# Conditional residual layer norm, 128 batches: the 1/standard-deviation chain in three VectorE steps instead of four, means made in pairs, the b2 row of ten more batches added by VectorE, and another order in the last five batches

## The chip, the core and the metric

The kernel runs on one core of a Trainium2 chip. The metric is the device time of one execution in microseconds (us). All work is in fp32, apart from three bf16 matmuls that only copy rows.

Engines: TensorE (PE in the profile, with PEld for its weight loads), VectorE (DVE), ScalarE (ACT), GpSimd (POOL). SP is the engine whose queue issues nearly all transfers.

## The reference

`x` has 128 batches of 128 rows by 512 columns. Each batch has an integer `language_id`, which picks one of ten sets of weights.

```python
w1 = W1[language_ids];  w2 = W2[language_ids]
h = relu(einsum('bsh,bha->bsa', x, w1) + b1[language_ids][:, None, :])      # 512 -> 128
adapted = einsum('bsa,bah->bsh', h, w2) + b2[language_ids][:, None, :]      # 128 -> 512
y = x + adapted
mean = jnp.mean(y, axis=-1, keepdims=True)
var = jnp.mean(jnp.square(y - mean), axis=-1, keepdims=True)
normed = (y - mean) * jax.lax.rsqrt(var + 1e-5)
out = x + normed * gamma[language_ids][:, None, :] + beta[language_ids][:, None, :]
```

## The kernel before

One batch is one tile of 128 partitions (its rows) by 512 columns. The weights of all ten languages stay on the chip. At the start one-row matmuls spread every row of `gamma`, `beta` and `b2` over the 128 partitions (`spread`), into `gamma_b`, `beta_b` and `b2_b`. The matrix `pick` selects the row, and its columns for `gamma` carry the factor 2.

One loop over `i` does all the work. Every engine gets its instructions in program order, because `keep` ties each to the one before it on its engine. In iteration `i`, with `b = i - 3`:

- PE transposes `x` of batch `i` (L231), multiplies batch `i-1` down to 128 columns (`down`, L254) and batch `i-2` up to 512 columns (`up`, L271, into the PSUM tile `py`). For some batches `up` is led by one bf16 matmul that writes the row of `b2` (L270).
- ACT copies the transposed tile to SBUF (`copy_xT`, L235), applies relu (L262), squares the residual tile of batch `b` with the sum of squares as by-product (`square`, L301), and copies the weights of a later batch into place (`stage_w1`, L222). After every odd batch it takes the square root for the pair (`deviation`, L312).
- POOL adds `b2` to `x` for most batches two ahead (`add_b2`, L241) and `beta` to `x` for every batch (`add_beta`, L248).
- DVE adds the residual, with the row sum as by-product (`residual`, L286), makes the negative mean (`negative_mean`, L292), and multiplies by gamma (`scale`, L335) and by 1/deviation while adding `x + beta` (`finish`, L344).

Where `b2` is added depends on the batch. `b2_by_matmul` names the batches where PE does it: 0 to 3, and those with `b % 4 == 1` that `b2_by_vector` does not take. `b2_by_vector` names those where DVE does it with one more instruction in front of the residual (L284): 13, 21, ..., 109. For all others POOL does it. That makes 22 batches for PE, 13 for DVE and 93 for POOL.

The reciprocal deviation of a pair takes ScalarE's root and one Heron step on DVE, in four instructions on tiles of two columns: `rstd_1` (L318, a reciprocal), `rstd_2` (L322), `rstd_3` (L326) and `rstd_4` (L330, a reciprocal). In an even step DVE runs `residual`, `rstd_1`, `scale` of the pair before, `negative_mean`, `rstd_2`, `finish` of an older batch, `rstd_3`. In an odd step it runs `b2` if it is its turn, then `residual`, `rstd_4`, `scale`, `negative_mean`, `finish`.

The tile pools set how far the engines can drift apart: `py` has five buffers, the transposed tile `pxT` one, the down product `ph` one.

The last five batches (from `E = 123`) are written out by hand in `tail`. There single batches replace pairs (`rstd_of`, `deviation_of`), two batches are finished by ACT and POOL (`by_pool`: ACT scales, POOL multiplies by gamma and adds; `shift` makes the bias that ACT needs), a third by ACT and POOL's last addition alone, and each store covers one batch (`store_last`).

Of the kernel before, what the change touches and what calls it, by code (L numbers as in the profile page):

```python
# [16 lines left out]
P = 128  # L17
# [8 lines left out]
def cond_resid_kernel(ctx: ExitStack, tc: tile.TileContext, x, itok, W1, b1, W2, b2, gamma, beta, out):  # L26
# [18 lines left out]
    def keep(ins):  # L45

        engine = ins.ins.engine
        if engine in last:
            tc.add_manual_dep(ins.ins, last[engine], behind, reason="kept order")
        last[engine] = ins.ins.name  # L50
        return ins
# [11 lines left out]
    p_y = ctx.enter_context(tc.tile_pool(name="p_y", bufs=5, space=PSUM))  # L63

    xs = {}

    def load_x(g):
        t = xp.tile([P, G, H], FP, tag="x", name=f"x_{g}")
# [26 lines left out]

    warm = const.tile([P, 1], FP, name="warm")
    keep(nc.vector.memset(warm, 1.0))
    keep(nc.scalar.activation(warm, warm, AF.Sqrt))
    def load_w1(k):
        keep(  # L100
            nc.sync.dma_start(out=w1[:, :, k, :], in_=W1[:, k * P : (k + 1) * P, :].rearrange("l p a -> p l a"))
# [15 lines left out]
    both = st.tile([P, R], FP, tag="both", name="both", bufs=1)[:96, :]  # L117
    keep(nc.vector.tensor_tensor(both, ident[:96, 0:R], ident[:96, 32 : 32 + R], ALU.add))
    keep(nc.vector.tensor_tensor(pick, both, ident[:96, 64 : 64 + R], ALU.add))
    keep(nc.vector.tensor_scalar(pick[:, L : 2 * L], pick[:, L : 2 * L], 2.0, None, ALU.mult))  # L120

    lids, w1s = {}, {}

# [7 lines left out]
    def lid(b, engine):  # L131
        g = b // G
        if (g, engine) not in lids:
            loads, vals = nc.values_load_multi_w_load_instructions(
                lang[0:1, g * G : (g + 1) * G],
                engines=[engine],
                min_val=0,
                max_val=L - 1,
                skip_runtime_bounds_check_because="clamped on the chip to 0..L-1 above",
            )  # L140
            for ins in loads:
                keep(ins)
            lids[g, engine] = vals
        return lids[g, engine][b % G]
# [66 lines left out]
    phs, pxs, sums = {}, {}, {}  # L211

    def b2_by_matmul(b):
        return b < 4 or (b % 4 == 1 and not b2_by_vector(b))

    def b2_by_vector(b):
        return b % 8 == 5 and 8 <= b < B - 16

    def stage_w1(b):
        w1s[b] = wp.tile([P, KC, A], FP, tag="w1s", name=f"w1s_{b}")  # L220
# [53 lines left out]
    def col(tiles, b):  # L274

        return tiles[b // 2][:, b % 2 : b % 2 + 1]

    def residual(b):
        r = rs.pop(b) if b in rs else xb(b)
        if b % 2 == 0:  # L280
            sums[b // 2] = st.tile([P, 2], FP, tag="sum", name=f"sum_{b // 2}")
        if b2_by_vector(b):
            v = lid(b, ET.DVE)
            keep(nc.vector.tensor_tensor(ys[b], ys[b], b2_b[:, bass.ds(v * H, H)], ALU.add))  # L284
        keep(
            nc.vector.scalar_tensor_tensor(ys[b], ys[b], 1.0, r, ALU.mult, ALU.add, accum_out=col(sums, b))  # L286
        )

    def negative_mean(b):
        if b % 2 == 0:  # L290
            nmeans[b // 2] = st.tile([P, 2], FP, tag="nmean", name=f"nmean_{b // 2}")
        keep(nc.vector.tensor_scalar(col(nmeans, b), col(sums, b), -1.0 / H, None, ALU.mult))  # L292

    def square(b):

# [7 lines left out]
            )  # L303
        )

    sds, y0s, stats = {}, {}, {}

    H3 = float(H) ** 3

    def deviation(g):  # L310
        sds[g] = st.tile([P, 2], FP, tag="sd", name=f"sd_{g}")
        keep(nc.scalar.activation(sds[g], ssqs[g], AF.Sqrt, bias=eps, scale=1.0 / H3))  # L312

    def rstd_1(g):
        y0s[g] = p_s.tile([P, 6], FP, tag="s", name=f"stat_{g}")
        keep(nc.vector.reciprocal(y0s[g][:, 0:2], sds[g]))  # L318

    def rstd_2(g):  # L320
        t = y0s[g]
        keep(nc.vector.scalar_tensor_tensor(t[:, 2:4], ssqs.pop(g), EPS * H3, t[:, 0:2], ALU.add, ALU.mult))  # L322

    def rstd_3(g):
        t = y0s[g]
        keep(nc.vector.scalar_tensor_tensor(t[:, 4:6], t[:, 2:4], 1.0 / H3, sds.pop(g), ALU.mult, ALU.add))  # L326

    def rstd_4(g):
        rstds[g] = st.tile([P, 2], FP, tag="rstd", name=f"rstd_{g}")
        keep(nc.vector.reciprocal(rstds[g], y0s.pop(g)[:, 4:6]))  # L330

    def scale(b):
        v = lid(b, ET.DVE)
# [17 lines left out]
    def on(b):  # L351
        return 0 <= b < B

    E = B - 5
    ends = {}

    def rstd_of(b, n):

        if not ends:
            ends["t"] = p_s.tile([P, 32], FP, tag="s", name="stat_ends")
        t = ends["t"][:, 8 * (b % 4) : 8 * (b % 4) + 3]
        if n == 1:
            keep(nc.vector.reciprocal(t[:, 0:1], sds[b]))
        elif n == 2:
            keep(
                nc.vector.scalar_tensor_tensor(t[:, 1:2], ssqs.pop(b), EPS * H3, t[:, 0:1], ALU.add, ALU.mult)
            )
        elif n == 3:  # L370
            keep(nc.vector.scalar_tensor_tensor(t[:, 2:3], t[:, 1:2], 1.0 / H3, sds.pop(b), ALU.mult, ALU.add))
        else:
            rstds[b] = st.tile([P, 1], FP, tag="rstd", name=f"rstd_{b}")
            keep(nc.vector.reciprocal(rstds[b], t[:, 2:3]))

    def deviation_of(b):
        ssq = st.tile([P, 1], FP, tag="ssq", name=f"ssq_{b}")
        sq = tp.tile([P, H], FP, tag="sq", name=f"sq_{b}")
        keep(nc.scalar.activation(sq, ys[b], AF.Square, bias=col(sums, b), scale=-float(H), accum_out=ssq))  # L379
        sds[b] = st.tile([P, 1], FP, tag="sd", name=f"sd_{b}")  # L380
        keep(nc.scalar.activation(sds[b], ssq, AF.Sqrt, bias=eps, scale=1.0 / H3))
        ssqs[b] = ssq

    def rstd_col(b):
        return rstds[b] if b > E else rstds[b // 2][:, b % 2 : b % 2 + 1]

    def shift(b):
        ends[b] = st.tile([P, 1], FP, tag="shift", name=f"shift_{b}")
        keep(nc.vector.tensor_scalar(ends[b], col(nmeans, b), rstd_col(b), None, ALU.mult))

    def by_pool(b, scaled):

        n = rp.tile([P, H], FP, tag="r", name=f"n_{b}")
        bias = 0.0 if scaled else ends.pop(b)
        keep(nc.scalar.activation(n, ys.pop(b), AF.Identity, bias=bias, scale=rstd_col(b)))  # L395
        if not scaled:
            keep(nc.gpsimd.tensor_tensor(n, n, gamma_b[:, bass.ds(lid(b, ET.Pool) * H, H)], ALU.mult))
        o = os[b // 2][:, b % 2, :]
        keep(nc.gpsimd.tensor_tensor(o, n, o, ALU.add))

    def store_last(b):
        nc.sync.dma_start(out=out[b], in_=os[b // 2][:, b % 2, :])

    def finish_last(b):
        o = os[b // 2][:, b % 2, :]
        keep(nc.vector.scalar_tensor_tensor(o, ys.pop(b), rstd_col(b), o, ALU.mult, ALU.add))  # L406
        store_last(b)

    def tail(b):
        p = E // 2  # L410
        if b == E + 3:
            rstd_of(b - 2, 3)
        residual(b)
        if b == E + 1:
            rstd_1(p)
            scale(E - 1)
            rstd_2(p)
            negative_mean(b)
            finish(E - 2)
            store(p - 1)  # L420
            rstd_3(p)
            deviation_of(b)
            rstd_4(p)
            shift(E)
            by_pool(E, False)
        elif b == E + 2:
            rstd_of(b - 1, 1)
            negative_mean(b)
            rstd_of(b - 1, 2)
            finish_last(E - 1)  # L430
            store_last(E)
            deviation_of(b)
        elif b == E + 3:
            rstd_of(b - 2, 4)
            shift(b - 2)
            residual(b + 1)
            by_pool(b - 2, False)
            store_last(b - 2)
            rstd_of(b - 1, 1)
            negative_mean(b)  # L440
            rstd_of(b - 1, 2)
            negative_mean(b + 1)
            scale(b - 1)
            deviation_of(b)
            rstd_of(b - 1, 3)
            rstd_of(b - 1, 4)
            scale(b)
            deviation_of(b + 1)
            by_pool(b - 1, True)
            store_last(b - 1)  # L450
            rstd_of(b, 1)
            rstd_of(b, 2)
            rstd_of(b + 1, 1)
            rstd_of(b, 3)
            rstd_of(b + 1, 2)
            scale(b + 1)
            rstd_of(b, 4)
            rstd_of(b + 1, 3)
            rstd_of(b + 1, 4)
            finish_last(b)  # L460
            finish_last(b + 1)


    def spin(n, width):
# [43 lines left out]
    for i in range(3, B + U):  # L508
# [35 lines left out]
        if b > E:  # L544
            tail(b)
        elif half == 0:
            if on(b):
                residual(b)
            if mine:
                rstd_1(p)  # L550
                scale(2 * p)
            if on(b):
                negative_mean(b)
            if mine:
                rstd_2(p)
            if old:
                finish(2 * p - 1)
                store(p - 1)
            if mine:
                rstd_3(p)  # L560
        else:
            if on(b):
                residual(b)
            if mine:
                rstd_4(p)
                scale(2 * p + 1)
            if on(b):
                negative_mean(b)
            if mine:
                finish(2 * p)  # L570
        if 0 <= b <= E:
# [46 lines left out]
```

## Time and profile before

| what | value |
|---|---|
| median of 3 runs | 312.11 us (312.1 to 312.15) |
| the profiled execution's own time | 311.92 us |
| its span, first to last instruction | 310.1 us |
| granted TensorE clock, mean | 0.988 |
| PE busy | 298.7 us, 96% of the span |
| DVE busy | 297.3 us, 96% |
| ACT busy | 280.3 us, 90% |
| POOL busy | 280.4 us, 90% |
| chain that ended last, by engine | PE 83%, DMA 8%, DVE 4% |

How to read it: a share of busy time counts time in which at least one instruction of the engine is open. An instruction's mean duration runs from its start to the end of its writes. On DVE and ACT the next instruction starts before that, so the distance between two starts in the timeline, not the duration, is what an instruction costs an engine that is full. The span plus about 1.8 us makes the time of the profiled execution.

### The profile page before, as it was taken

Reading aid. Unit: us, or ns where it says so; the run is one execution under the profiler, and the core shown is the slowest. Engines: PE = TensorE matmul, PEld = TensorE weight load, DVE = VectorE, ACT = ScalarE, POOL = GpSimd, SP = SyncE. Lnnn points to the kernel's source line nnn. Section 1 sums busy time; section 2 is a strip of 40 time slices with the busy share of each in tenths; the row PEclk is TensorE's granted clock in tenths of the full one; section 3 lists DMA queues with packets and bytes.
Section 4 is the critical chain, followed back from the end, with each engine's and each line's share of the span. In section 5 each row is a group of like instructions: output and inputs, shape, how many; then the busy total and the mean of one; then the engine's idle time right before and its main releaser. Section 6 shows DMA issues by size and latency. Waiting matters only on the chain.

```text
span 310.1 us, 7084 instructions
## 1 busy us (share of the span) xinstructions
PE 298.7 (96%) x1856; PEld 223.5 (72%) x1856; DVE 297.3 (96%) x945; ACT 280.3 (90%) x716; POOL 280.4 (90%) x234
## 2 busy tenths in 40 slices
PE   8999999999999999999999999999999999999970
PEld 3758778787777777777777777777777777777740
DVE  6778999999999999999999999999999999999995
ACT  3857999999999999999999999999999999999982
POOL 1349999999999999999999999999999999999963
PEclk9999999999999999999999999999999999999995
DMA  7999989975688667566876657577766766773234
GB/s 239 379 389 387 373 227 368 373 280 226 233 272 268 235 200 251 207 248 225 271 268 222 219 191 265 217 251 274 256 230 205 230 235 246 233 271 135 98 143 169
DMA packets 43481, 77.59 MB, mean 250 GB/s; under 512 B 1929, under 2 KB 7060, under 8 KB 43442
## 3 DMA queue, kind: packets, MB, share of 16 engines
q1 hardware_dynamic: 43382, 77.10, 71.7%
q8 instruction: 15, 0.25, 0.3%
q14 instruction: 24, 0.20, 0.2%
q10 hardware_dynamic: 60, 0.05, 0.1%
HBM read 43.58 MB, written 33.55 MB: 249 GB/s over the span
## 4 chain that ended last, share of the span: by engine, by line
PE 83%; DMA 8%; DVE 4%; ACT 1%; issue 1%; SPq 1%; DVEq 1%; ACTq 0%
PE ph L254 33%; PE py L271 32%; PE pxT L231 17%; DMA w1e<-in_L_cond_W_dram 4%; DMA x<-in_x_dram 3%; PE py L270 1%; DVE py L286 1%; DVE py L335 1%; DVE o L344 1%; SPq L152 1%; DMA ids<-in_itok_B_dram 0%; ACT sq L379 0%; DVEq L613 0%; ACT n L395 0%; DVE o L406 0%
## 5 line engine op out<-in xcount | busy, mean ns | idle before, releaser
L248 POOL TENSOR_TENSOR o<-x,beta_b 128x512 f32<-128x512 f32 x128 | 162.4, 1282 | 9.5 <-DVE beta_b L208 9.4
L254 PE MATMUL ph<-xT,w1s 128*128 128x128 f32 x1024 | 135.4, 275 | 0.0
L271 PE MATMUL py<-w,hT 128*128 x256 | 131.1, 594 | 0.0
L241 POOL TENSOR_TENSOR r<-x,b_b 128x512 f32<-128x512 f32 x93 | 119.1, 1281 | 12.5 <-DVE b_b L208 6.2
L254 PEld LDWEIGHTS ph<-xT,w1s 128*128 128x128 f32 x1024 | 125.0, 192 | 1.0 <-ACT hT L262 0.3
L231 PEld LDWEIGHTS pxT<-ident,x 128*128 128x128 f32 x512 | 66.7, 152 | 65.0 <-issue 46.4
L335 DVE SCALAR_TENSOR_TENSOR py<-py,nmean,gamma_b 128x512 f32<-128x512 f32 x126 | 93.7, 744 | 0.1
L344 DVE SCALAR_TENSOR_TENSOR o<-py,rstd,o 128x512 f32<-128x512 f32 x122 | 91.1, 747 | 0.0
L301 ACT ACTIVATE sq<-py,sum 128x512 f32<-128x512 f32 x124 | 84.8, 684 | 2.3 <-DVE py L286 2.1
L231 PE MATMUL pxT<-ident,x 128*128 128x128 f32 x512 | 77.9, 275 | 0.1
L235 ACT COPY xT<-pxT 128x512 f32<-128x512 f32 x128 | 74.9, 585 | 1.2 <-PE pxT L231 1.2
L286 DVE SCALAR_TENSOR_TENSOR py<-py,r 128x512 f32<-128x512 f32 x93 | 64.7, 695 | 1.1 <-POOL o L248 0.4
L222 ACT COPY w1s<-w 128x512 f32 x104 | 63.6, 612 | 0.0
L262 ACT ACTIVATE hT<-ph,b1T 128x128 f32<-128x128 f32 x128 | 47.1, 368 | 11.2 <-PE ph L254 7.8
L271 PEld LDWEIGHTS py<-w,hT 128*128 128x128 f32 x256 | 40.5, 192 | 2.4 <-issue 0.9
L286 DVE SCALAR_TENSOR_TENSOR py<-py,x 128x512 f32<-128x512 f32 x35 | 24.4, 697 | 2.0 <-issue 0.8
L301 ACT ACTIVATION_READ_ACCUMULATOR sq<-py,sum 128x1 f32 x124 | 25.2, 203 | 0.0
L312 ACT ACTIVATE sd<-ssq,eps 128x2 f32<-128x2 f32 x62 | 18.3, 296 | 2.1
L292 DVE TENSOR_SCALAR nmean<-sum 128x1 f32<-128x1 f32 x128 | 19.6, 153 | 0.1
L318 DVE RECIPROCAL stat<-sd 128x2 f32<-128x2 f32 x62 | 13.0, 210 | 1.5 <-ACT sd L312 1.5
L286 DVE DVE_READ_ACCUMULATOR py<-py,r 128x1 f32 x93 | 13.5, 145 | 0.0
L222 ACT COPY w1s<-w1e 128x512 f32 x16 | 9.8, 611 | 1.1 <-DMA w1e<-in_L_cond_W_dram 1.1
(56 smaller groups left out, 115.9 us busy)
## 6 DMA issues: line engine op xcount, KB each, us to landing
out_dram<-o SPq DMA_DIRECT2D x61, 512.0 KB, 3.3
x<-in_x_dram SPq DMA_DIRECT2D x29, 1024.0 KB, 6.2
x<-in_x_dram SPq DMA_DIRECT2D x6, 512.0 KB, 8.8
w1e<-in_L_cond_W_dram SPq DMA_DIRECT2D x2, 1280.0 KB, 11.5
w<-in_L_cond_W_dram SPq DMA_DIRECT2D x4, 640.0 KB, 7.9
w1s<-in_L_cond_W_dram SPq DMA_DIRECT2D x8, 256.0 KB, 8.4
w<-in_L_cond_W_dram SPq DMA_DIRECT2D x1, 1792.0 KB, 9.9
out_dram<-o SPq DMA_DIRECT2D x6, 256.0 KB, 2.0
```

The source lines that it names most:

```text
L222: keep(nc.scalar.copy(w1s[b].rearrange("p k a -> p (k a)"), src))
L231: keep(nc.tensor.transpose(pxs[b][:, k, :], cols, ident))
L235: keep(nc.scalar.copy(xT[b], pxs.pop(b)))
L241: keep(nc.gpsimd.tensor_tensor(rs[b], xb(b), b2_b[:, bass.ds(v * H, H)], ALU.add))
L248: keep(nc.gpsimd.tensor_tensor(os[g][:, j, :], xb(b), beta_b[:, bass.ds(v * H, H)], ALU.add))
L254: nc.tensor.matmul(phs[b], lhsT=w1s[b][:, k, :], rhs=xT[b][:, k, :], start=(k == 0), stop=(k == KC - 1))
L262: keep(nc.scalar.activation(hT[b], phs.pop(b), AF.Relu, bias=b1T[:, bass.ds(lid(b, ET.Activation), 1)]))
L271: keep(nc.tensor.matmul(ys[b], lhsT=hT[b], rhs=w2[:, bass.ds(v * H, H)], start=not m, stop=True))
L286: nc.vector.scalar_tensor_tensor(ys[b], ys[b], 1.0, r, ALU.mult, ALU.add, accum_out=col(sums, b))
L301: nc.scalar.activation(sq, ys[b], AF.Square, bias=col(sums, b), scale=-float(H), accum_out=col(ssqs, b))
L335: nc.vector.scalar_tensor_tensor(ys[b], ys[b], col(nmeans, b), gamma_b[:, bass.ds(v * H, H)], ALU.add, ALU.mult)
L344: nc.vector.scalar_tensor_tensor(o, ys.pop(b), rstds[g][:, j : j + 1], o, ALU.mult, ALU.add)
```

## The change

It has four parts.

1. ScalarE's function is `Abs_reciprocal_sqrt` instead of `Sqrt`, and writes into PSUM. The four DVE instructions of a pair become three (`rstd(g, 1..3)`, in `newton` and `newton_3`): with `t` the table's value and `v` the variance, `u = (ssq + eps)·t`, `u = u·t` with its scaling, `rstd = (u - 3)·t`. That is minus two times the Newton value, so `gamma` carries -0.5 instead of 2. The third instruction moves from the even step into the odd step, between DVE's `b2` addition and the residual.
2. `negative_means(g)` makes both negative means of a pair in one instruction in the odd step, in place of one `negative_mean` in each step. A column pair of zeros in PSUM is its second operand.
3. `b2` goes from PE to DVE for ten batches: 25, 41, 49, 57, 73, 81, 89, 105, 113 and 117. Batch 125 goes from PE to POOL. PE keeps 0 to 3, 5, 9, 17, 33, 65, 97 and 121 (11 batches); DVE has 23; POOL has 94.
4. In the last five batches the small operations come in another order, batch 125 is finished half by ACT and POOL (columns 0 to 255) and half by DVE (256 to 511), and each store is issued where its batch ends.

```diff
-    keep(nc.vector.tensor_scalar(pick[:, L : 2 * L], pick[:, L : 2 * L], 2.0, None, ALU.mult))
+    keep(nc.vector.tensor_scalar(pick[:, L : 2 * L], pick[:, L : 2 * L], -0.5, None, ALU.mult))
...
-        return b < 4 or (b % 4 == 1 and not b2_by_vector(b))
+        return b < 4 or (b % 4 == 1 and not b2_by_vector(b) and b < E)
...
-        return b % 8 == 5 and 8 <= b < B - 16
+        return b % 4 == 1 and (b % 8 == 5 if b < 24 else b % 32 != 1) and 8 <= b < B - 8
...
+    def smalls(lo, n):
+        if not small:
+            small["t"] = p_s.tile([P, 64], FP, tag="s", name="small")
+            keep(nc.vector.memset(small["t"][:, 0:2], 0.0))
+        return small["t"][:, lo : lo + n]
+
+    def negative_means(g):
+        nmeans[g] = st.tile([P, 2], FP, tag="nmean", name=f"nmean_{g}")
+        keep(nc.vector.scalar_tensor_tensor(nmeans[g], sums[g], -1.0 / H, smalls(0, 2), ALU.mult, ALU.add))
...
+    def root(ssq, t):
+        keep(nc.scalar.activation(t, ssq, AF.Abs_reciprocal_sqrt, bias=eps, scale=1.0 / H3))
+
+    def newton(n, ssq, t, u):
+        if n == 1:
+            keep(nc.vector.scalar_tensor_tensor(u, ssq, EPS * H3, t, ALU.add, ALU.mult))
+        else:
+            keep(nc.vector.scalar_tensor_tensor(u, u, 1.0 / H3, t, ALU.mult, ALU.mult))
+
+    def newton_3(rstd, t, u):
+        keep(nc.vector.scalar_tensor_tensor(rstd, u, -3.0, t, ALU.add, ALU.mult))
...
             if on(b):
                 residual(b)
             if mine:
-                rstd_1(p)
+                rstd(p, 1)
                 scale(2 * p)
-            if on(b):
-                negative_mean(b)
-            if mine:
-                rstd_2(p)
+                rstd(p, 2)
             if old:
                 finish(2 * p - 1)
                 store(p - 1)
+        else:
+            if on(b):
+                vector_b2(b)
             if mine:
-                rstd_3(p)
-        else:
+                rstd(p, 3)
             if on(b):
                 residual(b)
             if mine:
-                rstd_4(p)
                 scale(2 * p + 1)
             if on(b):
-                negative_mean(b)
+                negative_means(g)
             if mine:
                 finish(2 * p)
```

The end of the new `tail`, for batch 126 (`b`), with 125 as `b - 1` and 127 as `b + 1`:

```python
shift(b - 2); by_pool(b - 2, False); residual(b + 1); store_last(b - 2)
rstd_of(b - 1, 1); scale(b - 1); rstd_of(b - 1, 2); negative_means(b // 2)
deviation_of(b); scale(b); rstd_of(b - 1, 3); deviation_of(b + 1)
by_pool(b - 1, True, left)
rstd_of(b, 1); scale(b + 1); rstd_of(b, 2)
finish_cols(b - 1, right); store_last(b - 1)
rstd_of(b, 3); rstd_of(b + 1, 1); finish_cols(b); store_last(b)
rstd_of(b + 1, 2); rstd_of(b + 1, 3); finish_cols(b + 1); store_last(b + 1)
```

In `before` the same stretch was: `rstd_of(b - 2, 4)`, `shift(b - 2)`, `residual(b + 1)`, then after `scale(b)` of batches 125 and 126 one after the other all four small steps of 126 and 127 interleaved with `scale(b + 1)`, and the two `finish_last` at the end.

## Prediction

> **What bounds the kernel now.** I read the page's busy row first, then the groups by line, then the chain of waits, and last the timeline of each engine over one stretch of 5 us.
>
> ```profile
> PE 298.7 (96%) x1856; PEld 223.5 (72%) x1856; DVE 297.3 (96%) x945; ACT 280.3 (90%) x716; POOL 280.4 (90%) x234
> ...
> L270 PE MATMUL py<-parts,pick 96*128 96x512 bf16 x22 | 8.4, 381 | 0.5 <-DVE b_b L208 0.5
> ```
>
> Two engines are full, so a gain on either is capped by the other. The chain says which one leads, and what one `b2` matmul costs there:
>
> ```profile
> 144.49 0.89 PE ph L254 x8
> 145.38 0.22 PE py L270
> 145.60 0.86 PE py L271 x2
> 146.46 0.44 PE pxT L231 x4
> 146.90 0.89 PE ph L254 x8
> 147.79 0.86 PE py L271 x2
> 148.65 0.44 PE pxT L231 x4
> 149.09 0.89 PE ph L254 x8
> ```
>
> PE runs without a gap: a batch takes 2.19 (149.09 - 146.90), and 2.41 with L270. So L270 costs 0.22, not its mean duration of 0.381. DVE's timeline over the odd step of a batch whose `b2` it adds:
>
> ```profile
> 155.27 0.16 DVE L326 SCALAR_TENSOR_TENSOR stat<-stat,sd 128x2 f32<-128x2 f32 x1
> 155.34 0.69 DVE L284 TENSOR_TENSOR py<-py,b_b 128x512 f32<-128x512 f32 x1
> 156.06 0.70 DVE L286 SCALAR_TENSOR_TENSOR py<-py,x 128x512 f32<-128x512 f32 x1
> 156.68 0.14 DVE L286 DVE_READ_ACCUMULATOR py<-py,x 128x1 f32 x1
> 156.68 0.17 DVE L330 RECIPROCAL rstd<-stat 128x2 f32<-128x2 f32 x1
> 156.76 0.74 DVE L335 SCALAR_TENSOR_TENSOR py<-py,nmean,gamma_b 128x512 f32<-128x512 f32 x1
> 157.41 0.15 DVE L292 TENSOR_SCALAR nmean<-sum 128x1 f32<-128x1 f32 x1
> 157.47 0.74 DVE L344 SCALAR_TENSOR_TENSOR o<-py,rstd,o 128x512 f32<-128x512 f32 x1
> 158.13 0.69 DVE L286 SCALAR_TENSOR_TENSOR py<-py,r 128x512 f32<-128x512 f32 x1
> ```
>
> The distance between starts is the price. A small operation costs 0.06 to 0.08 (157.41 to 157.47; 156.68 to 156.76), whatever its duration of 0.15 to 0.21. Over the stretch from 60 to 280 us the odd step without L284 takes 2.05 and the even step 2.18, so a pair takes 4.235; L284 adds 0.727. A group of four batches with one L284 takes 9.20 on DVE and 8.76 on PE, and before the change such a group alternates with one that has L270 (8.47 on DVE, 8.98 on PE). Over eight batches that is 17.67 against 17.74: PE leads by a hair, and DVE waits for it at the residual. The third view is how lateness of DVE reaches PE:
>
> ```profile
> 156.86 0.69 ACT L301 ACTIVATE sq<-py,sum 128x512 f32<-128x512 f32 x1
> ...
> 158.38 0.58 ACT L235 COPY xT<-pxT 128x512 f32<-128x512 f32 x1
> ...
> 159.01 0.14 PEld L231 LDWEIGHTS pxT<-ident,x 128*128 128x128 f32 x1 [0.24 <-ACT xT L235]
> ```
>
> In that step the square waits for the residual (156.06 plus 0.61 plus the accumulator's 0.14) with only 0.04 to spare. Behind it in ACT's queue stands the copy of the transposed tile, and PE's next transposes wait for its one buffer: they start at 159.44, and their weight load of 0.14 was free at 159.01. So DVE may be late by about 0.3 (0.04 + 0.43 - 0.14 = 0.33, I take 0.31) when it begins such a step; beyond that PE stops.
>
> **PE.** Ten batches lose L270 to DVE, and 125 loses it to POOL. The first ten are worth 10 x 0.22 = 2.2; 125 is counted in the tail. POOL gets one more addition of 1.24 (start to start) at the end. It hides: POOL's last `beta` sum ends at 296.78, and it then idles 2.27 until 299.05.
>
> **DVE, small operations.** A pair loses one of its two means (0.06) and one of its four chain steps. The step that goes is the one behind the accumulator read, L330's place, worth 0.08 by the timeline; `rstd_3` only moves. A pair becomes 4.235 - 0.14 = 4.095; I take 4.105. What the trace cannot show is a `scale` directly behind an accumulator read, and there a rule of the Trainium skill speaks against the change. The row first: read and reciprocal start together (both 156.68), as if the read took no turn. "VectorE: DVE Perf Modes", section "Two Vector instructions with no wait between them", says an operation with accumulator output is two instructions; the same page's errata section gives an SBUF instruction about 58 cycles plus one per element at 0.96 GHz, some 0.06. By that the 0.08 is mostly the read's own turn and only 0.02 goes, for 0.08 a pair. I take the row and keep the rule as a rival. The new operations have the tile form of L322 and L326, so 0.06 each.
>
> **DVE, b2.** L284 to the residual is 0.727 because the residual reads what L284 wrote (0.691, its duration). Now `rstd(p, 3)` stands between them and fills 0.065 of the wait, so an addition costs 0.66. It stood ahead of L284 before; nothing else queues behind it except the residual and, through it, the square.
>
> **The balance.** A group with an addition is 2 x 4.105 + 0.66 = 8.87 on DVE against 8.76 on PE: DVE falls behind by 0.11 a group. A group that keeps L270 (33, 65, 97, 121) is 8.21 against 8.98 and makes up 0.77. In a run of seven groups (37 to 61, 69 to 93) the lateness at the start of the last is 6 x 0.11 = 0.66, so PE loses 0.66 - 0.31 = 0.35; twice that is 0.70. The run of five (101 to 117) loses 4 x 0.11 - 0.31 = 0.13; that of three (21 to 29) nothing. Together 0.83. PE keeps 2.2 - 0.83 = 1.4.
>
> **ACT.** The new function is a 128x2 operation in L312's place (0.296), at the same price. It writes into a PSUM bank that DVE also uses. The trace has no such sharing, and the second rule bears on it: "PSUM — Partial Sum Buffer", section "PSUM bank collisions raise a hardware error", has two engines on one bank kept apart by semaphores, so the root would also wait for `negative_means` of its step. That is ready 1.42 to 1.5 after the residual starts; the root comes no sooner than 0.80 (square) + 0.81 (157.67 - 156.86) = 1.6. By row and by rule the cost is nothing; without that cover of 0.1 it would be 0.1 in an additive step, with relu and the weight copy queued behind it. Bounds: 0 to 1 us in all; a gain is excluded, because the root ends on no chain. DVE's wait for the root (L318 in the next even step) had 0.18 to spare and keeps it.
>
> **Start.** The new zeros cost one small DVE instruction before batch 2, while the w1e transfer holds the chain until 31 us: nothing; without that cover, 0.06.
>
> **Tail**, from the residual of 124 (295.36) to the last `finish` (ends 306.82), walked with the same distances; where an operation reads the one just before it, 0.17 to 0.21 (L326 to L330, 297.49 to 297.68). Four places give time. (a) In the step of 124 one dependent reciprocal and one mean go, and PE's `up` of 125 comes 0.22 earlier: the residual of 125 starts 0.26 sooner (297.76). (b) `shift` of 124 no longer stands behind a late reciprocal, and relu of 127, queued on ACT behind the scaled copy of 123, moves too: the residual of 127 starts at 300.27 instead of 300.63. (c) From there DVE needed 6.19. Now: 0.61 residual, 0.08, `scale` 0.65, 0.07, 0.17 (means, read at once by the next), three small steps and two more big ones, half a `finish` 0.40, and two whole ones: `finish` of 127 starts 4.7 later and ends 5.4 later, at 305.7. So 1.1 is gained. (d) ACT keeps up: its root of 127 ends near 303.2, needed at 303.8. Half a copy and half a POOL sum end near 304.3, before SP reaches 125's store at 304.7 in its order; 126 and 127 stand behind that store, and 127 is ready last. From the last `finish` to the end the distance stays 310.1 - 306.8 = 3.3.
>
> **Sum.** 311.92 - 1.4 - 1.1 = 309.4 for the profiled execution, which lay 0.19 under the median; so 309.6.
>
> **The rivals.** *The read keeps its turn.* With 0.08 a pair saved, DVE needs 2 x 4.155 + 0.66 = 8.97 a group and falls behind by 0.21. PE loses 2 x (1.26 - 0.31) + (0.84 - 0.31) + (0.42 - 0.31) = 2.54, more than the 2.2. Only the tail remains, a gain of 0.8: 311.3. For it: the rule. Against: equal starts.
>
> *VectorE becomes the bound.* If only the mean's 0.06 comes free and the addition keeps its 0.727, a group is 2 x 4.175 + 0.727 = 9.08 and 0.32 late. PE then loses 2 x 1.61 + 0.97 + 0.33 = 4.5; less 3.3 it is 1.2 slower: 313.3. It decides from 0.25 a group. For it: two engines at 96% leave no room for seven more additions in 32 batches unless the small steps really pay. Against: the measured distances.
>
> *The tables do not go together.* The trace has one table load (L98, 1.283) for five functions. "ScalarE: Activation LUTs", section "What ACT_TABLE_LOAD costs", counts about 2.66 for every switch to another set. If root and square lay in different sets, two switches a pair would put over 130 us on ACT: near 450. The page says that cheap functions fill every set, so I give this little.
>
> **How the numbers follow.** The main case (309.6, itself 308.6 to 310.6) has 0.56, the read's turn 0.20, VectorE as bound 0.19, the tables 0.05. A measurement of this kernel can tell 0.2%, 0.6 us, from no change. Faster beyond that: all of the first and half of the second, 0.66. Within it: the other half and the mild end of the third, 0.12. Slower: 0.22. The range goes from 308.3 (no loss on PE, 2.2 + 1.1, and 0.5 for the tail's estimates) to 313.3, where the third case lies; it leaves out the tables and the worse half of the third.
>
> **What would show it.** L270 x11, L-lines of the `b2` addition x23; PE still at 2.19 a batch with idle time below 1 us; DVE pairs of 4.1 without and 4.77 with an addition. If `scale` starts more than 0.04 behind the accumulator read, the first rival holds. If PE's transposes start late more often than in the second half of each run of seven, the second. If the last `finish` comes later than 5.6 after the residual of 127, the tail is wrong. More than one ACT_TABLE_LOAD would overturn everything.

## The result, and the profile after

The changed kernel takes 311.27 us (median of 8 runs, 310.96 to 311.55), the kernel before 312.04 in the same comparison (8 runs, 311.69 to 312.15). The ratio is 0.9976, with a 95% interval of 0.9965 to 0.9987. That is 0.77 us faster, where 2.5 was forecast: the sign is right and the size is not.

The page of the changed kernel, and its rows for the three operations that the change is about:

```profile
PE 298.0 (96%) x1845; PEld 222.1 (72%) x1845; DVE 296.2 (96%) x827; ACT 280.1 (91%) x716; POOL 281.4 (91%) x235
```

```profile
L289 DVE SCALAR_TENSOR_TENSOR py<-py,r 128x512 f32<-128x512 f32 x94 | 65.1, 693 | 1.4 <-PE py L272 0.7 <-POOL r L242 0.2
...
L282 DVE TENSOR_TENSOR py<-py,b_b 128x512 f32<-128x512 f32 x23 | 15.9, 692 | 0.0
...
L303 DVE SCALAR_TENSOR_TENSOR nmean<-sum,small 128x2 f32<-128x2 f32 x64 | 9.7, 151 | 0.1
...
L271 PE MATMUL py<-parts,pick 96*128 96x512 bf16 x11 | 4.2, 380 | 0.4 <-DVE b_b L209 0.4
```

Eleven `b2` matmuls are gone, VectorE runs 827 instructions instead of 945 although ten additions (L282) have come, and both engines still show 96%. Busy shares do not tell the two kernels apart here; distances between starts do. Line numbers have moved: the residual is L289, `scale` L355, `finish` L364, `up` L272, the table operation L322, the three Newton steps L326, L328 and L331. The timeline of VectorE over the odd step with an addition (batch 61):

```profile
155.41 0.69 DVE L282 TENSOR_TENSOR py<-py,b_b 128x512 f32<-128x512 f32 x1
156.01 0.15 DVE L331 SCALAR_TENSOR_TENSOR rstd<-part,small 128x2 f32<-128x2 f32 x1
156.14 0.70 DVE L289 SCALAR_TENSOR_TENSOR py<-py,x 128x512 f32<-128x512 f32 x1
156.75 0.14 DVE L289 DVE_READ_ACCUMULATOR py<-py,x 128x1 f32 x1
156.75 0.76 DVE L355 SCALAR_TENSOR_TENSOR py<-py,nmean,gamma_b 128x512 f32<-128x512 f32 x1
157.42 0.15 DVE L303 SCALAR_TENSOR_TENSOR nmean<-sum,small 128x2 f32<-128x2 f32 x1
157.48 0.74 DVE L364 SCALAR_TENSOR_TENSOR o<-py,rstd,o 128x512 f32<-128x512 f32 x1
158.14 0.69 DVE L289 SCALAR_TENSOR_TENSOR py<-py,r 128x512 f32<-128x512 f32 x1
```

The last Newton step (156.01) fills the gap ahead of the residual, as expected: from L282 to the residual it is 0.73 (156.14 - 155.41), where the kernel before needed the same 0.727 and a small operation of 0.066 ahead of it. What TensorE does in this step and what VectorE does at its end (the first two lines are the `up` of the batch before, for comparison):

```profile
155.91 0.30 PEld L272 LDWEIGHTS py<-w,hT 128*128 128x128 f32 x2
156.02 1.02 PE L272 MATMUL py<-w,hT 128*128 x2
...
157.31 1.06 PE L255 MATMUL ph<-xT,w1s 128*128 128x128 f32 x8
...
157.48 0.74 DVE L364 SCALAR_TENSOR_TENSOR o<-py,rstd,o 128x512 f32<-128x512 f32 x1
...
158.28 0.30 PEld L272 LDWEIGHTS py<-w,hT 128*128 128x128 f32 x2
158.28 1.12 PE L272 MATMUL py<-w,hT 128*128 x2
```

The down product occupies TensorE for 0.89, until 158.20. The weights of the `up` product, which in the step before load 0.11 ahead of their turn (155.91 and 156.02), load at 158.28, and so does the matmul start. The product then takes 1.12 instead of 1.02. VectorE's `finish` ends at 157.48 + 0.74 = 158.22. The `up` is that of batch 63, the `finish` that of batch 58, and `py` has five buffers: TensorE waits for the buffer. VectorE sets the pace.

The whole trace shows the same. Take the distance between the starts of one `up` and the next, less 2.19, or less 2.41 where a `b2` matmul lies between them: for batches 22 to 123 what is left adds up to 1.72 us of lost time. All of it lies in ten places, in the last four groups of each run of seven and in the last two of the run of five. A typical place loses 0.07 before the `up` and 0.10 behind it. In the kernel before, the same sum is zero.

Where the time went, by stage (starts of the residuals and of the last `finish`):

| stretch, us | before | after | forecast of the change |
|---|---|---|---|
| residual of 20 to residual of 124 | 230.96 | 230.49 | -1.4 |
| residual of 124 to the start of the last `finish` | 10.72 | 10.47 | -1.1 |

The first row gave 0.47 and the second 0.25. Their sum, 0.72, is nearly all of the change of the spans (310.1 to 309.4).

### The profile page after: what moved, and what is told of

Its sections match the earlier page's. It is cut to its first block, busy times and chain, and to the rows that moved or that the text cites. A ratio compares the mean times of both kernels' runs of the same rounds, so it can differ in the third digit from the quotient of the medians.

```text
span 309.4 us, 6966 instructions
## 1 busy us (share of the span) xinstructions
PE 298.0 (96%) x1845; PEld 222.1 (72%) x1845; DVE 296.2 (96%) x827; ACT 280.1 (91%) x716; POOL 281.4 (91%) x235
## 5 line engine op out<-in xcount | busy, mean ns | idle before, releaser
L272 PE MATMUL py<-w,hT 128*128 x256 | 132.0, 598 | 0.0
L355 DVE SCALAR_TENSOR_TENSOR py<-py,nmean,gamma_b 128x512 f32<-128x512 f32 x126 | 95.0, 754 | 0.1
L364 DVE SCALAR_TENSOR_TENSOR o<-py,rstd,o 128x512 f32<-128x512 f32 x122 | 91.0, 746 | 0.0
L289 DVE SCALAR_TENSOR_TENSOR py<-py,r 128x512 f32<-128x512 f32 x94 | 65.1, 693 | 1.4 <-PE py L272 0.7
L272 PEld LDWEIGHTS py<-w,hT 128*128 128x128 f32 x256 | 39.6, 191 | 2.8 <-issue 0.9
L289 DVE SCALAR_TENSOR_TENSOR py<-py,x 128x512 f32<-128x512 f32 x34 | 23.8, 699 | 1.4 <-issue 0.8
L322 ACT ACTIVATE small<-ssq,eps 128x2 f32<-128x2 f32 (+1 forms) x66 | 17.5, 265 | 2.3 <-DVE nmean L303 0.2
L282 DVE TENSOR_TENSOR py<-py,b_b 128x512 f32<-128x512 f32 x23 | 15.9, 692 | 0.0
L289 DVE DVE_READ_ACCUMULATOR py<-py,r 128x1 f32 x94 | 13.3, 142 | 0.0
L326 DVE SCALAR_TENSOR_TENSOR part<-ssq,small 128x2 f32<-128x2 f32 x62 | 9.4, 152 | 1.8 <-ACT small L322 1.8
```

Of the source, the lines that this page charges most:

```text
L272: keep(nc.tensor.matmul(ys[b], lhsT=hT[b], rhs=w2[:, bass.ds(v * H, H)], start=not m, stop=True))
L355: nc.vector.scalar_tensor_tensor(ys[b], ys[b], col(nmeans, b), gamma_b[:, bass.ds(v * H, H)], ALU.add, ALU.mult)
L364: nc.vector.scalar_tensor_tensor(o, ys.pop(b), rstds[g][:, j : j + 1], o, ALU.mult, ALU.add)
```

## The experiments

The theories were: the longer of two sums, VectorE's distances or TensorE's, sets the time between batches 24 and 121 (A, later D); the division of `b2` or the shorter chain carries the gain by itself; VectorE's lateness reaches TensorE through ScalarE's queue, as the prediction had it, or through the `py` buffers.

**The old division of b2, all else of the change.**

```diff
-        return b < 4 or (b % 4 == 1 and not b2_by_vector(b) and b < E)
+        return b < 4 or (b % 4 == 1 and not b2_by_vector(b))
...
-        return b % 4 == 1 and (b % 8 == 5 if b < 24 else b % 32 != 1) and 8 <= b < B - 8
+        return b % 8 == 5 and 8 <= b < B - 16
```

> The changed kernel, but with the rows of b2 divided as before (22 batches on TensorE, 13 on VectorE, 93 on GpSimd); the shorter 1/deviation chain, the paired means and the new tail stay. Theory A (the new division gains little because VectorE, late by about 0.17 us per group of four, stops TensorE): with the old division TensorE leads and loses nothing, but takes its 22 matmuls; what remains is some 0.2 us of the first 24 batches and 0.1 to 0.2 us of the tail, so 311.6 to 311.8 us, 0.3 to 0.5 below before. Rival B (the division carries the whole gain, the shorter chain none): 312.0, equal to before. Rival C (the division only costs): below 311.0.

Measured: 311.94 against 311.91 before, ratio 0.9997 (0.9988 to 1.0006). The forecast of a small gain missed. Its 104 batches took 231.06 instead of 230.96: the shorter chain and the paired means do nothing where TensorE leads. The tail's gain is there (10.46 instead of 10.72), but in the profiled execution the first 20 batches took 0.15 longer. Its page has DVE at 94% (292.6 us), nearly 5 us less than before, and PE unchanged at 298.8.

**The new division, all else as before.**

> The kernel before, with only the new division of b2 (11 batches on TensorE, 23 on VectorE, 94 on GpSimd); the four-step chain, the single means and the old tail stay. Theory D (between batches 24 and 121 the longer of two sums sets the time: VectorE's distances or TensorE's): VectorE's group of four with an addition takes 2 x 4.235 + 0.73 = 9.20, and 21 of those and three without one (8.47) make 218.6 us, against 212.9 on TensorE before: some 5 us slower, 316.5 to 317.5. Rival B (the division is worth its 10 x 0.22 on TensorE whatever VectorE does): 310.

The edit is the same pair of lines in the kernel before, the other way round. Measured: 318.07 (4 runs), ratio 1.0194 (1.0178 to 1.0209): 6.1 us slower. So the first of the two parts alone gives nothing and the second alone costs much; only together do they gain. The chain that ended last, 83% TensorE in the kernel before, is here 37% VectorE and 30% TensorE.

**TensorE takes b2 in one batch of 16.**

```diff
-        return b % 4 == 1 and (b % 8 == 5 if b < 24 else b % 32 != 1) and 8 <= b < B - 8
+        return b % 4 == 1 and (b % 8 == 5 if b < 24 else b % 16 != 1) and 8 <= b < B - 8
```

> The changed kernel with b2 by TensorE in one batch of 16 instead of one of 32 from batch 24 on (33, 49, 65, 81, 97, 113, 121): three matmuls more on TensorE, three additions fewer on VectorE, runs of three additive groups instead of seven. Theory A: VectorE falls behind by 0.17 to 0.18 us a group, 0.35 at the start of a run's last group, below the 0.39 from which TensorE stops; TensorE then keeps 7 x 0.22 = 1.5 us instead of the 0.3 it kept between batches 24 and 124: 310.0 to 310.3 us, 1.0 to 1.2 below the changed kernel. Rival B (VectorE's lateness does not reach TensorE, and the missing time is elsewhere): three matmuls more cost 3 x 0.22 = 0.66: 311.9.

Measured: 310.04 (5 runs, 309.87 to 310.41), ratio 0.9938 (0.9925 to 0.9952). Giving TensorE three matmuls back makes the kernel 1.2 us faster than the changed one. Its stretch from 20 to 124 takes 229.40, which is 1.56 under before: seven matmuls saved at 0.22 are 1.54, all of it kept. Its page:

```profile
PE 296.3 (96%) x1848; PEld 221.9 (72%) x1848; DVE 294.8 (96%) x824; ACT 280.2 (91%) x716; POOL 281.2 (91%) x235
```

**The weight copy ahead of the square.**

```diff
+        early = b2_by_vector(b) and i + 1 >= FIRST and on(i + 1)
+        if early:
+            stage_w1(i + 1)
         if 0 <= b <= E:
             square(b)
...
-        if i + 1 >= FIRST and on(i + 1):
+        if i + 1 >= FIRST and on(i + 1) and not early:
```

> The changed kernel; in the steps in which VectorE adds b2, ScalarE copies the next weights before the square instead of after it. Theory A (the late residual reaches TensorE through ScalarE's queue: square, then the copy of the transposed tile, for which TensorE's transposes wait): the weight copy of 0.50 us (start to start) now lies ahead of the wait, so VectorE may be late by 0.39 + 0.5 = 0.9 us; a run of seven loses 6 x 0.175 - 0.9 = 0.15 instead of 0.66, the run of five nothing instead of 0.3: 1.2 to 1.3 us less, 310.0 to 310.2 us. Rival B (VectorE holds TensorE through the five py buffers, or through relu): the order on ScalarE does not matter, 311.2 to 311.4. Rival C (the root comes 0.5 later and VectorE waits for it): slower than 311.5.

Measured: 311.20, ratio 0.9978 (0.9968 to 0.9987): the changed kernel's time, as rival B had it, so theory A's path falls. The edit did take ScalarE's waits for a late residual away, as the lists of waits of the changed kernel and of this one show (total, times, longest):

```profile
ACT sq L312 <- DVE py L289: 6.1, 15, 2.0
...
ACT sq L312 <- DVE py L289: 2.1, 1, 2.1
```

But TensorE still loses 1.64 us by the sum above, at the same ten places. The timeline of the same step shows why:

```profile
156.45 0.61 ACT L223 COPY w1s<-w 128x512 f32 x1
...
156.96 0.69 ACT L312 ACTIVATE sq<-py,sum 128x512 f32<-128x512 f32 x1
...
157.28 1.06 PE L255 MATMUL ph<-xT,w1s 128*128 128x128 f32 x8
...
157.45 0.74 DVE L364 SCALAR_TENSOR_TENSOR o<-py,rstd,o 128x512 f32<-128x512 f32 x1
...
157.97 0.58 ACT L236 COPY xT<-pxT 128x512 f32<-128x512 f32 x1
...
158.24 0.30 PEld L272 LDWEIGHTS py<-w,hT 128*128 128x128 f32 x2
158.24 1.13 PE L272 MATMUL py<-w,hT 128*128 x2
```

The copy of the transposed tile now comes at 157.97 instead of 158.45, and still `up` starts at 158.24, 0.05 behind the end of `finish` (158.19). The buffer is the place where VectorE's lateness lands.

**The finish ahead of scale, and the weight copy ahead of the square.** In the odd steps with an addition `finish(2 * p)` moved in front of `scale(2 * p + 1)`.

> The changed kernel; in the steps with a b2 addition, VectorE's finish of the older batch stands ahead of scale and the means instead of behind them, and ScalarE copies the weights before the square. Theory D with the place found in the trace (TensorE's up product waits for the py buffer that this finish frees): the buffer comes free 0.73 us sooner and ScalarE's path has 0.5 more to spare, so VectorE may be later by 0.4 to 0.5 us before TensorE stops. But VectorE's sum over 32 batches (7 x 8.94 + 8.27 = 70.9) stays above TensorE's (70.3), so the gain comes once and not in every run of seven: 310.7 to 311.0 us. Rival (the buffers are the bound, not VectorE's sum): 310.0.

Measured: 311.48, ratio 0.9987 (0.9978 to 0.9996). It gained nothing, so this expectation missed, and its rival (310.0) too. The edit brought a wait of its own, in the list of waits of this kernel:

```profile
ACT small L322 <- DVE nmean L303: 8.4, 19, 0.8
```

The table's operation on ScalarE waited for the means, 19 times and up to 0.8, because both touch the PSUM tile with the zeros and the table's values, and the means now came last. The `py` buffer, though, no longer holds TensorE:

```profile
157.04 0.75 DVE L364 SCALAR_TENSOR_TENSOR o<-py,rstd,o 128x512 f32<-128x512 f32 x1
...
158.47 1.02 PE L272 MATMUL py<-w,hT 128*128 x2
```

The `finish` of 58 ends at 157.79, 0.68 ahead of the `up` of 63; between batches 24 and 123 no `up` starts less than 0.24 behind its `finish`. Nearly all of VectorE's groups with an addition still take 8.93 to 8.94 between residuals, as in the changed kernel. TensorE loses 1.83 at the same ten places, now ahead of its transposes, and the trace puts that wait down to ScalarE's copy. So the buffer is where VectorE's lateness lands in the changed kernel, but freeing it brings nothing while VectorE's own sum is the longer one: the lateness comes by another way.

**The root of 127 behind the Newton step of 126, in the tail.**

```diff
-            deviation_of(b + 1)
-            by_pool(b - 1, True, left)
             rstd_of(b, 1)
+            deviation_of(b + 1)
+            by_pool(b - 1, True, left)
```

> The changed kernel, in the tail only the first Newton step of batch 126 moved ahead of the square and root of batch 127 in program order. Theory A (in the tail VectorE's step for 126 waits for the root of 127, which it does not need, because both touch the PSUM tile that holds the table's values): the wait of 0.45 us before that step goes, and the last finish comes 0.45 to 0.5 earlier: 310.8 us. Rival B (it waits for the root of 126 itself or for ScalarE's queue): nothing changes, 311.3; or ScalarE's root of 127 now waits for VectorE and the gain is given back, 311.2 to 311.4.

First the changed kernel's timeline at that place:

```profile
301.41 0.26 ACT L322 ACTIVATE small<-ssq,eps 128x1 f32<-128x1 f32 x1 [0.17 <-DVE nmean L303]
...
302.41 0.27 ACT L322 ACTIVATE small<-ssq,eps 128x1 f32<-128x1 f32 x1
...
302.71 0.15 DVE L326 SCALAR_TENSOR_TENSOR part_of<-ssq,small 128x1 f32<-128x1 f32 x1 [0.45 <-ACT small L322]
...
302.83 0.76 DVE L355 SCALAR_TENSOR_TENSOR py<-py,nmean,gamma_b 128x512 f32<-128x512 f32 x1
```

The value for 126 is there at 301.67 (301.41 + 0.26). VectorE's step for 126 starts at 302.71, when ScalarE has written the value for 127 (302.68), which stands before it in program order and in the same PSUM tile. With the edit:

```profile
302.31 0.15 DVE L326 SCALAR_TENSOR_TENSOR part_of<-ssq,small 128x1 f32<-128x1 f32 x1
302.33 0.19 ACT L395 ACTIVATION_READ_ACCUMULATOR sq<-py,sum 128x1 f32 x1
302.55 0.27 ACT L322 ACTIVATE small<-ssq,eps 128x1 f32<-128x1 f32 x1
302.56 0.76 DVE L355 SCALAR_TENSOR_TENSOR py<-py,nmean,gamma_b 128x512 f32<-128x512 f32 x1
```

No wait is left there, and from the residual of 124 to the last `finish` it takes 10.04 instead of 10.47. But the time hardly follows: 311.08, ratio 0.9973 (0.9962 to 0.9984), 0.0003 from the changed kernel and inside both intervals. From the start of the last `finish` to the end of the span it now takes 4.42 instead of 4.03.

**Both of these edits.**

> The changed kernel with TensorE taking b2 in one batch of 16 and with the first Newton step of 126 ahead of the root of 127: both of the edits that gained by themselves (1.2 and 0.2 us against the changed kernel). Theory D: they lie in different stretches and add up: 309.7 to 309.9 us. Rival: the tail is paced by something that starts from TensorE's end, and the second edit gives nothing on top: 310.0 to 310.1.

Measured: 310.09 (5 runs), ratio 0.9943 (0.9930 to 0.9957), no better than with the division alone. The rival holds in its outcome: the tail's 0.4 is given back behind the last `finish`. The windows of this kernel show where, in the last two columns:

```profile
core 0: us, PE busy (x) PEld busy (x) DVE busy (x) ACT busy (x) POOL busy (x), PEclk, DMA share, GB/s
...
302.00:304.00 2.00, 0.00 (x0) 0.00 (x0) 1.81 (x9) 0.04 (x1) 1.53 (x2) 0.75 0.14 54
304.00:306.00 2.00, 0.00 (x0) 0.00 (x0) 0.63 (x1) 0.00 (x0) 0.00 (x0) 0.50 1.01 377
```

Between 304 and 306 us the DMA engines are full. The stores of 124 to 127 are issued at 302.88, 303.56, 303.98 and 304.66. Each carries 256 KB, 0.70 us at 377 GB/s, and the first waits for POOL's last sum of 124. In the changed kernel that sum is the first of the two additions in this line:

```profile
302.71 1.94 POOL L413 TENSOR_TENSOR o<-n,o 128x512 f32<-128x512 f32 x2
```

It ends at 303.97, and the store of 124 is issued at 304.00. From that issue to the end of the span it takes 5.36 there, 5.32 with the tail edit alone and 5.31 here. So the last stretch runs from POOL's sum of 124 through four transfers, and an earlier `finish` on VectorE does not shorten it.

**The half of 125 stored by itself.** In this version the half that VectorE finishes goes first, ahead of the store of 124.

```diff
-            store_last(b - 1)
+            store_last(b - 1, right)
+            store_last(b - 2)
+            store_last(b - 1, left)
```

> The kernel with b2 by TensorE in one batch of 16 and the reordered tail, in which the last finish came 0.4 us earlier but the time did not fall; the two halves of batch 125 are now stored separately, the half that VectorE finishes first and ahead of the store of 124. Theory F (the stores of 124 to 127, 256 KB each at some 380 GB/s, run one behind the other at the end and now set it): 128 KB move into a stretch in which the DMA engines were idle, the end comes 0.25 to 0.35 sooner: 309.75 to 309.85 us, and the distance from the start of the last finish to the end falls from 4.32 to about 4.05. Rival (the end is set by the store of 127 alone and the missing time is noise): 310.05 to 310.1, distance 4.3.

Measured: 310.23 (5 runs), ratio 0.9942 (0.9929 to 0.9956); from the last `finish` to the end 4.53. The remedy failed, because the edit did not do what it was meant to do. VectorE's half is ready at 302.49, but its store is issued only at 302.77, 0.03 behind the end of POOL's sum of 124 (302.74), just as the first store is in the other versions. The list of what SP waited for names POOL's sums (total, times, longest), and the longest of these waits is the one up to 302.74:

```profile
SPq L416 <- POOL o L413: 4.4, 3, 2.1
```

Why the half store waited for it was not tested; 124 and 125 share one output tile. So no bytes moved into the idle stretch, and the same bytes took longer in five pieces (the share of busy DMA engines falls to 0.5 twice within the burst). That the burst is full is shown; that a better order would shorten it is not.

**The means from SBUF alone.**

```diff
-        keep(nc.vector.scalar_tensor_tensor(nmeans[g], sums[g], -1.0 / H, smalls(0, 2), ALU.mult, ALU.add))
+        keep(nc.vector.tensor_scalar(nmeans[g], sums[g], -1.0 / H, None, ALU.mult))
```

> The kernel with one batch of 16 on TensorE and the reordered tail, and the paired means as a tensor_scalar on SBUF alone, without the zeros in PSUM. Theory E (an instruction that reads PSUM starts later behind one that writes PSUM, which is why scale to the next start takes 0.664 instead of 0.648): the distance from scale to the means in the odd step falls to 0.648, that in the even step (to a Newton step that reads PSUM) stays 0.664; in the tail nothing on VectorE but the Newton steps guards the bank, so the root of 126 no longer waits 0.17 for the means. Time equal to the kernel without this edit or 0.1 less: 309.6 to 309.8. Rival (scale itself is longer, whatever follows): both distances stay 0.664.

Measured: 347.26 (5 runs), ratio 1.1137 (1.1122 to 1.1152): 37 us slower than the kernel of both edits (310.09), from which it differs by this one instruction. The expectation missed, and the distance from `scale` to the means stayed at 0.663, so theory E falls; its rival, that `scale` itself is longer whatever follows, fits. The group:

```profile
L303 DVE TENSOR_SCALAR nmean<-sum 128x2 f32<-128x2 f32 x64 | 52.1, 814 | 0.1
```

And four lines of its timeline:

```profile
162.98 1.26 POOL L249 TENSOR_TENSOR o<-x,beta_b 128x512 f32<-128x512 f32 x1
164.00 0.27 DVE L303 TENSOR_SCALAR nmean<-sum 128x2 f32<-128x2 f32 x1
...
168.13 1.29 POOL L242 TENSOR_TENSOR r<-x,b_b 128x512 f32<-128x512 f32 x1
168.25 1.19 DVE L303 TENSOR_SCALAR nmean<-sum 128x2 f32<-128x2 f32 x1
```

The instruction of two columns ends 0.02 to 0.03 behind the end of a POOL addition both times (164.27 against 164.24, 169.44 against 169.42), however late it came; so it is in 62 of the 64 cases. With the zeros in PSUM it takes 0.151.

## Why the prediction was wrong, point by point

**The steps that failed.** Two terms of the sum were mis-sized. In the loop it was the saving on VectorE's small operations: the prediction took 0.13 a pair ("A pair becomes 4.235 - 0.14 = 4.095; I take 4.105"), and 0.10 was measured. That took TensorE's loss from 0.83 to 1.7 us. In the tail it was (c) and (d): a last `finish` 4.7 behind the residual of 127, with the distance to the end unchanged. It came 5.57 behind. The 3.3 from its end to the end of the span held in the changed kernel, but grew by 0.39 when an edit brought the `finish` 0.43 forward.

**The cause in one table.** For batches 36 to 100 (16 groups of four) the two sums can be made from measured distances. TensorE: 8.76 a group and 0.22 for each `b2` matmul. VectorE with the old chain: 9.20 for a group with an addition and 8.47 without; with the new chain 8.93 (2.797 + 2.003 + 2.137 + 1.997 between residuals) and 8.27 (two pairs of 4.135).

| kernel | VectorE's sum | TensorE's sum | measured, residual 36 to 100 |
|---|---|---|---|
| before (8 additions, 8 matmuls) | 141.4 | 141.9 | 141.99 |
| new chain, old division (8, 8) | 137.6 | 141.9 | 141.84 |
| old chain, new division (14, 2) | 145.7 | 140.6 | 145.90 |
| the change (14, 2) | 141.6 | 140.6 | 142.04 |
| one in 16 by TensorE (12, 4) | 140.2 | 141.0 | 141.08 |

Each measured time is the larger sum, within 0.2 us, except the change, which stands 0.4 above it. The distances come from the kernel before and from the changed kernel itself, so the other three rows are the test. In the change VectorE also waits a little for TensorE: after each group without an addition it has caught up, and the last step of that group and the first of the next take some 0.2 longer than VectorE needs. The change moved the bound from TensorE to VectorE and gained almost nothing between these batches.

The prediction's own figures had no reserve for this. Over a period of eight groups they give 7 x 8.87 + 8.21 = 70.3 on VectorE and 7 x 8.76 + 8.98 = 70.3 on TensorE. With 8.93 and 8.27 VectorE's sum is 70.8. The rival "VectorE becomes the bound" was nearest in kind; it had this case decide from 0.25 a group, and 0.17 was enough to take 1.7 of the 2.2.

**Small operations, the term that was mis-sized.** Between residuals a pair without an addition takes 2.137 + 1.997 = 4.135, against the 4.235 from which the working started. The parts: the mean's place in the even step gave 0.045 (forecast 0.06). The step in front of `scale` (L330's place) was costed at 0.08. From the accumulator read to the instruction behind `scale` it took 0.730 (0.082 + 0.648); without the step it takes 0.664, so 0.066 went. Both fall short for one reason: `scale` takes 0.664 to the next start in the changed kernel and took 0.648 before, twice a pair. The prediction left that distance as it was. The step in L322's place also takes 0.073 instead of 0.063. A group with an addition is therefore 8.93 and not 8.87, and VectorE falls behind TensorE's 8.76 by 0.17 instead of 0.11. Put into the prediction's own formula this makes 2 x (6 x 0.17 - 0.31) + (4 x 0.17 - 0.31) + (2 x 0.17 - 0.31) = 1.8 instead of 0.83; the two stages of the result say 2.2 - 0.47 = 1.7. An error of 0.03 in a pair, over the 50 pairs of the loop, came to 0.9 us.

**The accumulator read.** The rival that the read keeps its turn is not what the trace shows: in the changed kernel `scale` starts with the read (both 156.75 above). The longer `scale` is not the read's doing either: in the even steps a Newton step stands between the read and `scale`, and the distance behind `scale` is 0.664 there too. By luck the rival's 311.3 is the time measured, with other terms: it put all of its gain into the tail.

**The way to TensorE.** The prediction put it through ScalarE's square and the one transposed buffer, and set the margin at 0.31. In the changed kernel it is the `py` buffer that a late `finish` frees. That wait was not priced at all, although the five buffers stood in the description. In a step with an addition `finish` ends 0.66 later than in others, and that uses up most of its margin. A run of seven loses 0.70 (four places of 0.17 to 0.18), so the margin that fits is 6 x 0.175 - 0.70, about 0.35. That the wrong place had nearly the right size was luck; the copying order then showed that it was the wrong place.

**The b2 addition** cost 0.66 net (0.60 + 0.13 - 0.065) as forecast, and **TensorE's matmul** 0.22: both confirmed, the second by the version with seven fewer.

**The tail.** (a) and (b) were right: the residuals of 125 and 127 come 2.40 and 4.90 behind that of 124, as walked (2.40 and 4.91). The walk failed in (c) and (d). The last `finish` starts 5.57 behind the residual of 127, not 4.7; in the kernel before it was 5.45, so this stretch grew instead of shrinking. (The prediction's own sign of a wrong tail, later than 5.6, was set too wide to show it.) Of the excess, 0.43 is the wait for a root that the step did not need. The prediction weighed the rule of the Trainium skill on a shared PSUM bank ("PSUM — Partial Sum Buffer", section "PSUM bank collisions raise a hardware error") for the main loop, found it covered there, which held (ScalarE waited 0.2 in all for the means, in the tail), and did not apply it to the tail, where two roots and four Newton steps share the tile. The tile's order in the program is then an order in time. The rest are waits of about 0.1 to 0.2 each that the walk left out: `scale` of 127, for one, starts only behind ScalarE's square of the tile that it overwrites (302.56, behind a square that ends at 302.43, in the version with the edit). Finally (d): it took the end for the last `finish` and 3.3 more, which held in the changed kernel by chance. SP's order does not hold the last store, but the four transfers follow each other without a gap from POOL's sum of 124 on, and where VectorE ends earlier they set the end. In the changed kernel the two ways end within 0.05 of each other: from the first of the four stores to the end it takes 5.36, and 5.31 or 5.32 where the stores set the end. So (c) alone could have brought next to nothing.

**The start, the tables, the root's price:** no cost, as forecast. There is one table load (L99, 1.283), so the two functions go together, and the table operation took 0.265 instead of 0.296. The rival on the tables was priced too low by its own figure: two switches a pair at 2.66 each make an estimated 330 us over 62 pairs, not 130.

**What stays open:** why `scale` takes 0.664 to the next start; how much of the 0.4 us between the change and its larger sum deeper buffers could bring; and whether an earlier sum of 124 on POOL, or another order of the last stores, would bring the tail's 0.4 to the end.

## What to carry to other kernels

When two engines are equally full, add up the distances between starts for each engine over one full period of the schedule, before and after: here the larger sum gave the time within 0.4 us in 142. A change that moves work from one engine to the other is worth at most what the point brings where the two sums are equal, not the work removed. By the sums that point lies near 13 additions and 3 matmuls in 64 batches. The version with 12 and 4 gained 1.56 us in the loop; with 14 and 2, past the point, 1.1 of them were lost. A tile that two engines share for unrelated small values turns program order into waiting; look for it in hand-ordered stretches first. At the end of a kernel ask which engine's result the first of the last stores waits for: here it was POOL's, and VectorE's last instruction came earlier in vain.

## What the runs showed of the hardware that was not expected

A `tensor_scalar` from SBUF to SBUF of two fp32 columns took 0.814 on average and in 62 of 64 cases ended 0.02 to 0.03 behind a running POOL instruction. The one of a single column (L292 of the kernel before) took 0.153, and the same arithmetic on two columns with one operand in PSUM 0.151. In the same kernel the difference was 37 us. That POOL is what the instruction waited for was not tested by itself.

An accumulator read took no turn of its own on VectorE: between 60 and 280 us the next instruction, large or small, shows the same start in all 99 cases of either kernel.

A wait of 0.07 on TensorE cost 0.17: the `up` that waited for its buffer had its weights loaded at its own start and not 0.11 ahead, it took 1.12 instead of 1.02, and the transposes behind it started 0.96 instead of 0.86 after it. The added 0.10 was the same with the weight copy ahead of the square, and where the wait was 0.35 (the kernel before with the new division).
